# Four graph layers on one core: the source exponentials kept tile-innermost, their rows stored in one transfer and awaited head by head, with a new order table

## The chip, the cores and the metric

The kernel runs on one core of one Trainium2 chip, as one program. The time is the device time of that core in microseconds (us). An execution is timed as a whole; the profile comes from one profiled execution of the same program.

## What is computed

The input `x` is 16 graphs of 1024 nodes with 256 features, all float32, and one 1024 x 1024 adjacency matrix. Four layers follow each other, each as `x = x + layer(relu(layernorm(x)))`. Three of them (0, 1 and 3) are graph attention layers; layers 0 and 1 have one head of 256 features, layer 3 has four heads of 64. Layer 2 is a transformer block of eight heads of 32 features over the same mask, with two layer norms and a feed-forward part.

```
Wh = h @ W;  e_src = Wh @ a1;  e_dst = Wh @ a2
e   = leaky_relu(e_src[:, None] + e_dst[None, :], alpha)      # 1024 x 1024 per graph and head
att = softmax(where(adj > 0, e, -big), axis=-1)
out = elu(att @ Wh)                                            # layer 0: relu
```

The kernel never forms the exponential of a 1024 x 1024 matrix in these layers. Since the leaky relu is a maximum of two linear functions, `exp(e)` is, up to a factor that cancels in the softmax, `max(r[query], e2[key]) * e3[key]`, where `r`, `e2` and `e3` are exponentials of one number per node. `r` comes from the source part of the node ("source exponentials"), and the other two from its destination part.

## The kernel before

**Work units.** A "stage" is one layer of one graph, 64 in all. Nodes stand in `NT` = 8 tiles of 128 partitions. The stages are interleaved in a fixed list (`order`): in the middle of the run the cycle is layer 2 of graph b, layer 1 of graph b+1, layer 3 of graph b, layer 0 of graph b+2. While one stage does its main products on TensorE (PE), the next one is prepared.

**The way in.** For each tile: statistics of the norm (VectorE, DVE), the reciprocal root on GpSimd (POOL: `root`, L1051 and L1074), the normalised tile (ACT or DVE), then for every four tiles a PE transpose (`transpose_rows`, L1090) that ACT copies to `hT` (L1093). Products of `hT` with the weights follow on PE (`project`, L1097: `gat_values`, `two_values`, `queries_keys`).

**The source exponentials.** In an attention layer with H heads the product of a tile carries 3H extra columns; ACT turns them into exponentials in `e` (L1222, L1233), laid out as tile, then column: `e[p, t, c]`. `sources` then brings the rows `r` to all partitions: PE transposes `e` with its 8 x 3H columns (`tpr`, L1294), DVE copies the result to `rows_sb` (L1298), SyncE (SP) stores the H rows of `r` per tile to DRAM (`kept`; L1306 one transfer in one-head layers, L1309 eight transfers in layer 3), and SP loads them back, each row broadcast to 128 partitions (`r`; L1320 two halves of one row, L1325 four whole rows, two to a buffer). Only the first stage goes another way.

**The weights and the products.** DVE makes the weights `p = max(r, e2) * mask` (L1362, 512 queries for one-head layers; L1443, 1024 queries in layer 3, two heads to a pair), PE multiplies them with the values (L1379; in layer 3 `pair_item` with L1477 for values and L1501 for the sums). In layer 3 the weights of a pair of heads wait for one operation that loads both heads' rows. Layer 2 (`dot_item`) makes scores on PE (L1597), exponentials on ACT (L1611), the mask on DVE (L1619), values on PE (L1628), and adds two tiles of weights by a transfer of 1 MB that POOL issues (`gather`, L1645) before PE sums them (`totals`, L1658). POOL also issues the adding of constant rows in DRAM to `y` and `x` (`offset`, L1733); DVE's `finish` (L1797) waits for that of `y`.

**The order of the work.** The program records some 12,000 operations with their engine, an assumed cost, the operations they follow and the buffers they take and free. `play` then lays them out on five engines (and on a sixth line that stands for POOL's transfer queue) by a list scheduler: of the operations that could start soon, the one with the lowest key goes first. The key of each operation is read from `RANKS`, three characters to an operation, if its length is three times the number of operations; otherwise the program computes keys itself. What comes out is one fixed order of instructions for each engine, which the chip runs with semaphores between engines. So the assumed costs and `RANKS` decide only the order; they take no time on the chip.

**Shapes of products on PE.** Operations carry a `form`: 132 for the scores (32 rows of the array), 32 for products into 32-column parts (L1628, L1658, L1477, L1501), none for the rest. PE is slower by a fraction of a microsecond where two neighbours differ in form, and the scheduler's `SWITCH` stands for that.

Of the kernel before, what the change touches and what calls it, by code (L numbers as in the profile page):

```python
# [26 lines left out]
F32 = mybir.dt.float32  # L27
# [12 lines left out]
H2 = 8  # L40
# [7 lines left out]
    "#pO##/#29$4?#/<#._#28$Km#-d#9d#1K#/V#Yt#%>#$h$?-#+7#$u##6#(,#&-#$p#%O##O$As#;U#%U##.#$R#&L#,|$3z#':#-2#_.#'G#XJ"  # L48
    "$+<#'}#(o#)o#*I#)7#)<#*M#*e#$c$&3#$.#$P#UX#a@#$Q#qf$KH#$[#qV$,K##5#$6$?k##7#$>#*)#%=#$W#%Y#$T#$'#$w#'0#$@#%|#$n"
    "#$e$/]#$##$g$EX$A{#$i#qN#$L#${#ky#$($DA$H?#%/##:#&i$5&##J#%:#&P#%+#|w#%%#$l$#3#%@#`&#?m#i[##Y#$;#'&$4b#.n#lu#/m"  # L50
    "#Ns#Z1#)#$Mo#)x#N_#/g#,/#{(#'r#+/#(V#%{#$q#$Z##y##D#%$#$|#%N#&o#&y#-%#&O#$1#&H$9|##i#(1#Y:#-/#&F$+>#&w$:u#p1#(Y"
    "#%X#%W#%r$4R#'+#64#|-#'P#zk#&t#%M$Nz##}$NA$BA#)z#%o#'[#&X#XI#`a#*G$JF#(##+d#2Y#2C#d3#%a#%s#&D#&+#&G#&`#&Q#&7#%["
    "#%]#'g$7(#(K#*`$Ce#([#&f#']##m$NW#'>#*_$4<#'C#';#(J#%e#3}#&4#`8$@l#(Z#%w#&a#%.#1o#&]#.w#C[#/r#'Q#*z#(5#)C#-}#*F"
    "$=R#%V#'%$=^$.3#nf$K>#C0#%?#&J#z%#'W#)[#'X$EU$4[#'l#t)$4d#&=##;$2I#&?#)6$JX#Ag$4_#&##,5#&c$9.#(_#&:#$/#&k#(r#%5"
    "#[C#Z0#*H$>g#&g#rv$:-#&n#&|#-R#'($<P#6}#&;#)e#.t#%`#>o#%}#mY#&U##[#mt#'.$NG#&T#$*#%n$4J#&S$-($Ny#s6#IV#&s#*P#)]"
    "#m9$AU#(2##8#%0#$z#&3#&M#%T#$%$I##'8#/c#N$#*b#`J$Ds$L6#'/#v2#$m#4[#/Z#N'#<f#/B#'4#'v#'H#4<#Z>#)j$'9$J|##s#(&$L5"
    "#(S#Nz#+*$'8#'@#@o#)b#&h#(}#*4#*,#>w$+b#(s$M|#)k#,+#q+#%x#&6#'b#'m#Z?#(Q#(0#(T#)*#%K#o^#%J#*&$CO#+<#)$#)S$L=$&#"
    "#)P#*x$Di#H-$+^#l<#%##(t#&l#$}#<2#G`$.V$,.#$d#$]#&@#;_$C.##<#(^#(z#)/#E0#%6#$-#zs#$D#*6#,-#+K#,j#0n#:O#(U$@x#AU"
    "#yu#(/#)T#'J#'1#%)#(A#'M#&m#%*#kq$.6#qH$:m$5C#cs#9P$LP#m3#(.$5]$MO#UI#io$*]$8-#&(#(W#U|#/?#U:#'x$Cw$8*#)>#(G#]6"
    "#IN#UD$Ms#<9#,3#@R#{)#*E#Fq#)=$9C#)u#R2#EI#F-$7h$8t#q`$#^#GC#Gv#(v#)^#[x#$,##I$;V#SC#R=#)A#*}#$k#$&#]O$&H#T+$8i"  # L60
    "#Vy#)3##F$3c#@4#G;#0z#h$#(7#){#Jd#Fr#j=#K8$Eq#Fx#*B$-D#*3#+@#+e$G4#+E#gp#`[#.:#-$#)X#19#-x#0E#0F#)d#**#Y3#F?#F}"
    "#F3$EC#lb#*S#*@$@*#<<#Z=#mN#0K#<?#*##*$#*p#<=#Jc#Ft#0O#)p#)9#)}#W2#UG#y.#L[#1c#}h#*l#8O#.,##C#+L#*V#12#'t#^(#*="
    "#2d#hd#,A$IW#]h#ha#*^#*2#+x#V:#)8#)f#):$4I#(|#*n#`_#4M#,##51#0J#)|#+%#+9#)+#?C#`=#,x#UH#4+#*:#+:#&{#,h#&W#j%#*k"
    "#1D#+,$,d#.s$$[#,Q$Cr#Ol$3q#*U#Hg#)M$1?#+o#+i#+&#+>#c8#)W#lD#,W#+F#v%#,Z#*s#56#(L#/'$C>#+v#+w#*v#E|$EH#DE#,;#+H"
    "#e8#,m#+h#+0#E{#*A#<N#,`#,<$:W#d=#Y0#D`#+|$%,#13#-@#,9#Xb#d<#.N$+j#,k#,D#kK#D_#kJ#*K#,r$Ov#Im#Pm#-_#,K$)q#p@#ZP"
    "#0q#,s#,O$'*#0'$'x#p`#-P#qo#0]#-L#-,$)B#nX$)_#/+#-]#,w$)r#>0$,P#0i#-b$':#q8#+W#-O#b*#M8$+S#>/#+=#-N$(<$-w$'s#0w"
    "#,6#)h$1b#%p#+I#c^$)N#r$$-y#)V#+c$,1#1'#|v#'5#HJ#Th#qQ$2M#*Y$3@#,8#96#+s#(]#,d#+R#(a#.E#'7#-X#n##-5#q4#-f$H.#-B"
    "#%8#/S$>?#.h#&5#=/$I`#0V$-<#(<$4z#<S#ur#08#X]#'h#/k#^B$+&#$0#2%#XC$*i#9T#yy$(*#(;#0f#.O$Ba$B4#=y$5?#,^#bD$D.#*7"
    "#)I#5/#15#.u#9%#0e#/H#/=#{c$Bp#K>#0M#SK#vm$2U$0W#14#m_$0b#SN#}Y#Eu#2G#@W#2S#O]#,.#*C#?w#k|#1I#.T#-.$>V#jg#&r#8["
    "#em#pk#OQ#*O#-E#+N#iA#$4#>h#.*#.C$=M#'U#'B#hf#$?#&'#dq#.i#,>#_2#>R##4#'c#-V#$C$$x#'S$%?#)s#/:#8.#@w#0R#-8#,p#,o"  # L70
    "#,g#*{#0:#-^#_1#)l#^^#&x#/*#%g$32#e*#/x#*R#,e#-w#}m#./#.W#/E#`?#)Z#`>#-[#/(#&*$2N#0p#.5$B##'z#$9#.##.+#0d##P#-j"
    "$KI#-Y#0v#$V#mJ#1/#01#%l#-`#%R#.{#/{#0)#]q#:2#kX#:1#/X#(=$5;#1@#.-$>v#Lg#%q#:Y#0H#/w#$U#.z#0A#.y#1y$3f#92#Az#Oi"
    "#+t#RW#,7#(`#.A#06#,&#/F#0D#2+#.|#,u#0P##H#1?#u<#/,#4K#0r#.o#*w#2,#G4#=+#7>#u)#4:#]b#(B#uS#6V#@J#@+#7?#03#,Y#+6"
    "#-S#-s$Eu#4]#zH#=*#$j#.b#,2#9m#<o#}R#}c#+z#-m#Om#+k#&^#.V#'q$'&#0{#xk#+l#.r#1$$#'#CA#(E#+g$:l$3_#/##)i#/>#AA#3>"
    "#(@#.q#3#$/f#WR#2-#[{#W_#/^#BE#C|#6/$/w#)c$Cd#QZ#*]#,E#@;#*|#+u#?^#+1#+Z#;?#,:$Cv#,S#)Y#)n#-4#*r#lJ#3B#,q$)3#+C"
    "#(H$')$,@#qk#Pv#Id$Hj$&.#'e#+A$7m#.R#e0#0%#ta#->#,N#+G#,i$&{#&)#;Z$'+#)U$'(#-1#t:#+5$(n#&u#0G$(a$G6$%+#-o#Zg#7X"
    "#9F#9E#/O#-(#.7#/I#/2#0.#04#d%#YC#SR#1P#-y#??#@N#-k#HC$,3#Qc#00#=A##U$1;$-B$3)#7@#7U#4J#@Y#/A#/$#F##/Q$/F#7]#xs"
    "#=x#+b#'T#0|#*L#|B#.0#Wo#R%#uc#1F#1>$*D$MF$M6$6z#jr$?j#U<#/R$5[#/|#.U#-7#$E#0##B/#_G$2?#2]$/p#q3#W=$8?#W;##u#MK"
    "$FZ$/o#C>$;w$*?$*>$;j$/l$D$$,Q#d,#^h$)F$73#-M#.M#Jl#1G#cn#[5#QV#GQ$I]#/u$/u#0j$>w$C]$Nb#*i$M5$FE#D^#co#QK#1m#_|"
    "#6[#6L#^9#[##-G#^j#S6#MV#m*#/[#*d#-a#A,#7%#/z#/a#0x#-;#N{#6Z#-n#/Y#0S#.p#LF#3-#4c#4H#2<$DP#1%#1w#1Q#hg#5L#3F#1z"  # L80
    "#8C#0k#1A#0t#0>#44#4)#2F#3S#/G#1|#1u#02#1:#4=#0*#2E#1e#2e#5B#3q#1U#5D#3D$AE$3[#3I#4,#4##Bp#3E#C;$3o#Tz#L9#G<#ah"
    "$4|#Ge#,$#1V#4q#4S$%%#5C#3T#2'#2c#G##,y#4E$MY#'Y$:I#3<#1j#2W#1S#2D#F*#d[#2{#/h$#M#3j#E*#dd#Oo$:H#2v#3Z#3h#;f$A*"
    "#QW$/_#dO#i0$37#2h#Gs#18#Qo$Bm#2q#37#2r#r]#5c#O|#2H#4y#2u#O/#9.$G=$8@#Vq#lx$81#2w#R[#ux#LC$&h#to#1+#1Z#V|#*m$(:"
    "#mw$4v#?V$EW#3=#xi#h;#mn$8P#oH#$v##X#hh#dp#+M#n=#e|#Pe#8##$a#/%$8O#rR$4a#jV#$b##n#h6#rS$8L#n)#3k#P?$Ek#4Y##k#z'"
    "#oG$4$$0j#4w#3P#.=#jT#2I#jK#5@$3E#RS$BP#4$$LL#2s#u&#2n#49#$J#2b#2p#5-#2f#3G#1x#5*#PF#4s#Yk#5N#1R#6>#0b#5T#Tv#76"
    "#1&#6r#@}#U0$EE#*t#wT#:)$%*$#.#73#4_#Vn#&[#4m#2|#N&$-m#9##`E#/n#6X#Nq$J8#/0#/9#5Y$J:#22#;(#2}#?>#31#?=$'0#5;#Ac"
    "#[g#9Q#R>#'^#[$#9Z#5:#]5#^=#ny#Yq#EU#l;#Z8#6O#jL#5.#Z9#^m#@k##'$CS#k?#z&#>r#3$#4g#48#?[#23#N/#4;#PG$E2#4z##(#4-"
    "#;#$CK$N(#5'#4R#0[#LV#1[$(6#3_#Q&#s:#3s#3;#6H#KT$@7$'r#4?#0?$@;$Mi$5n#:@$G3#Pj$Ec#S,#3a$M/#')#17#u'#4/#4b#|r$Mh"
    "$@:#4d#Pc#0/#0g#7}#7;#3d$)##5z#cb#5^$FA#5U#Fv#4C#|z#6,$GB#XQ$Dp#[3#5s$3g#6-$2X#5Z#34#);#2k#69#f+#6?#$I#Z6$Au#5t"
    "#$N#79#6e#-##5)#6|#Rh#zx#6p#n2#7(#6a#$+#bQ#[e#5v#e{$#Y#3*#6o#5u#6Y#/3#eD#0+#7##6&#0<#XN$EJ#[6#9+#8w$7p#3&#wf#6`"  # L90
    "#-Z#6C#71$&D#9V#]Y#6s$(7#7k#5o#3/$L2#4|#Y^#4O#TZ#:b#]H#42#Yg#d(#c[#3x#vx#4A#7e#=B#6F#5J#68$*S#3]#4X#e3#:B#7L#7="
    "#&e#4o$In#4e#7c#8r#5O#6:#5##6j#fu#5+#|H#5X#8e#5d#5M$Io#0`#2R#5F#3g#8^#4T#7b#3{#tE#M^$A@$@X#:$#VP#4u#5f#J`$(3$Al"
# [527 lines left out]
def fast_path(tc, bad, x, adj, l0_w, l0_a, l1_w, l1_a, w_qkv, ln1_g, ln1_b, ln2_g, ln2_b, w1, b1, w2, b2, l3_w, l3_a, out):  # L620
# [13 lines left out]
    with ctx:  # L634
# [357 lines left out]
        class Stage:  # L992
# [38 lines left out]
            @property  # L1031
            def e(self):
                return self.eh.t

            @property
            def y(self):
                return self.yh.t
# [1006 lines left out]
```

## Time and profile before

| | |
|---|---|
| median of 3 runs | 4192.47 us (4190.18 to 4197.8) |
| profiled execution, as timed | 4190.34 us |
| its span, first to last instruction | 4188.6 us |
| mean granted TensorE clock | 0.995 |
| PE busy | 4085.4 us, 98% |
| DVE busy | 3174.7 us, 76% |
| ACT busy | 2319.6 us, 55% |
| POOL busy | 1207.9 us, 29% |
| transfers | 398.96 MB, 95 GB/s in the mean |

The span and the time as run differ by 1.7 us, and the profiled execution lies 2.1 us below the median. "Busy" counts an engine from the start to the end of each instruction; a PE that is busy may still be slowed by its clock, by a change of form or by a wait inside an instruction. In the profile a wait is put down to the engine that released it last.

### The profile page before, as it was taken

To read this page: it belongs to the slowest core of one execution; us is meant where nothing else is said; L and a number is where in the kernel's file an instruction comes from. 1 tells how busy PE (TensorE), PEld (TensorE's weight loads), DVE (VectorE), ACT (ScalarE), POOL (GpSimd) and SP (SyncE) were. 2 spreads that over 40 slices of the span, in tenths; PEclk is the share of its full clock that TensorE was granted. 3 is DMA by queue.
4 is the path that set the end of the run, shared out by engine and by line. 5 is a ranking of instruction groups with operands and counts; after the bars stand their busy time and mean duration, and the time that the engine had idled before them with its cause. 6 is when DMAs were issued, how large, how long until landed. Compare 5 with 4: busy or idle time off the path is not lost. (4 is left out here: it accounts for less than half of the span.)

```text
span 4188.6 us, 67542 instructions
## 1 busy us (share of the span) xinstructions
PE 4085.4 (98%) x25993; PEld 2158.0 (52%) x25993; DVE 3174.7 (76%) x5964; ACT 2319.6 (55%) x4235; POOL 1207.9 (29%) x2025
## 2 busy tenths in 40 slices
PE   8999999999999999999999999999999999999998
PEld 7735364553545535465454654536555365555433
DVE  7487867778676787777877778786787867768688
ACT  5564655646465464654647556474564645665452
POOL 2314231413314232141322313223142231423231
PEclk9999999999999999999999999999999999999999
DMA  3181914518154181641716327172361723554361
GB/s 125 31 167 31 186 36 106 106 46 171 36 126 97 37 170 41 132 95 46 156 37 149 79 63 144 31 166 62 78 130 51 162 46 90 114 113 98 85 122 47
DMA packets 106826, 398.96 MB, mean 95 GB/s; under 512 B 11528, under 2 KB 47744, under 8 KB 73728
## 3 DMA queue, kind: packets, MB, share of 16 engines
q0 software_dynamic: 46080, 302.01, 36.7%
q1 hardware_dynamic: 60000, 92.03, 6.7%
q8 instruction: 206, 3.38, 0.3%
q14 instruction: 124, 1.02, 0.1%
q10 hardware_dynamic: 416, 0.52, 0.0%
HBM read 107.87 MB, written 18.21 MB: 30 GB/s over the span
## 5 line engine op out<-in xcount | busy, mean ns | idle before, releaser
L1619 DVE TENSOR_TENSOR pe<-pe,mask 128x1024 f32<-128x1024 f32 x1024 | 1201.4, 1219 | 201.4 <-ACT pe L1611 196.8
L1611 ACT ACTIVATE pe<-sc 128x1024 f32<-128x1024 f32 x1024 | 996.4, 1023 | 322.2 <-PE sc L1597 241.0
L1379 PE MATMUL av<-v,p 128*128 128x257 f32 x4096 | 951.9, 382 | 10.2 <-ACT o L1402 6.0
L1379 PEld LDWEIGHTS av<-v,p 128*128 128x128 f32 x4096 | 761.6, 190 | 191.6 <-issue 48.7
L1443 DVE SCALAR_TENSOR_TENSOR p<-r,e,mask 128x1024 f32<-128x1024 f32 x512 | 623.1, 1274 | 121.7 <-DMA r<-kept 98.5
L1597 PE MATMUL sc<-qT,kT 32*128 32x512 f32 x4096 | 619.8, 640 | 5.1 <-ACT pm L1071 4.3
L1628 PE MATMUL acc<-pe,v 128*32 128x512 f32 x4096 | 539.9, 603 | 9.1 <-DVE pe L1619 6.1
L1074 POOL TENSOR_SCALAR rstd<-stats 128x1 f32<-128x1 f32 x512 | 166.6, 325 | 1157.9 <-ACT xn L1071 695.6
L1645 POOL DMA_DIRECT2D pe<-pe x256 | 224.9, 880 | 952.0 <-PE acc L1628 632.7
L1477 PE MATMUL acc<-p,v 128*32 128x512 f32 x4096 | 464.3, 595 | 0.0
L1597 PEld LDWEIGHTS sc<-qT,kT 32*128 32x128 f32 x4096 | 190.6, 183 | 379.7 <-issue 164.8
L1362 DVE SCALAR_TENSOR_TENSOR p<-r,e,mask 128x512 f32<-128x512 f32 x512 | 347.7, 742 | 30.5 <-DMA r<-kept 27.1
L1097 PE MATMUL pm<-l_wx,hT 128*128 128x259 f32 (+1 forms) x1536 | 366.6, 388 | 3.6 <-ACT hT L1093 3.0
L1075 POOL TENSOR_TENSOR rstd<-rstd,minus_half 128x1 f32<-128x1 f32 x512 | 331.9, 648 | 42.7
L1097 PEld LDWEIGHTS pm<-l_wx,hT 128*128 128x128 f32 x1536 | 286.2, 190 | 78.6 <-ACT hT L1093 13.3
L1658 PE MATMUL sums<-pe,pick 128*32 128x512 f32 x2048 | 268.5, 600 | 21.1 <-DMA pe<-pe 20.6
L1477 PEld LDWEIGHTS acc<-p,v 128*32 128x32 f32 x4096 | 129.8, 110 | 301.3 <-issue 288.8
L1628 PEld LDWEIGHTS acc<-pe,v 128*32 128x32 f32 x4096 | 96.6, 108 | 346.0 <-issue 200.8
L1051 POOL TENSOR_SCALAR rstd<-stats 128x1 f32<-128x1 f32 x256 | 138.5, 541 | 441.7 <-DVE stats L1048 438.7
L1501 PE MATMUL sums<-p,e 128*32 128x512 f32 x2048 | 242.3, 593 | 0.0
L1097 PE MATMUL pm<-hT,qkv_sb 128*128 128x512 f32 x512 | 228.0, 594 | 2.9 <-ACT hT L1093 2.8
L1052 POOL TENSOR_TENSOR rstd<-rstd,minus_half 128x1 f32<-128x1 f32 x256 | 221.8, 866 | 21.3
(122 smaller groups left out, 4147.9 us busy)
## 6 DMA issues: line engine op xcount, KB each, us to landing
pe<-pe POOLq DMA_DIRECT2D x256, 1024.0 KB, 8.8
r<-kept SPq DMA_DIRECT2D x64, 512.0 KB
x<-in_x_dram SPq DMA_DIRECT2D x32, 512.0 KB
x<-offsets POOLq DMA_DIRECT2D x32, 512.0 KB, 5.6
y<-offsets POOLq DMA_DIRECT2D x32, 512.0 KB, 6.9
out_dram<-x SPq DMA_DIRECT2D x64, 256.0 KB
r<-kept SPq DMA_DIRECT2D x62, 256.0 KB
edges<-in_adj_dram SPq DMA_DIRECT2D x8, 512.0 KB
```

Of the source, the lines that this page charges most:

```text
L1075: nc.gpsimd.tensor_tensor(rh.t, rh.t, minus_half, ALU.pow)
L1097: nc.tensor.matmul(dst, lhsT=lhsT[:, k, :], rhs=rhs[:, k, :], start=(k == 0), stop=(k == KC - 1))
L1362: nc.vector.scalar_tensor_tensor(ph.t[:, j % each, :], rh.t, s.e[:, j, H + h : H + h + 1], mask[:, j, cols], ALU.max, ALU.mult)
L1379: nc.tensor.matmul(avh.t[:, : s.hs + 1], lhsT=phs[part].t[:, j % each, i * P : (i + 1) * P], rhs=s.v[:, j, h, :], start=(j == 0), stop=(j ...
L1443: nc.vector.scalar_tensor_tensor(ph.t[:, hh, :], s.rh[hp].t[:, hh, :], s.e[:, j, col : col + 1], mask[:, j, :], ALU.max, ALU.mult)
L1477: nc.tensor.matmul(acc[n].t[(2 * hh + part) * W : (2 * hh + part + 1) * W, :], lhsT=s.v[:, jj, h, part * W : (part + 1) * W], rhs=p, start ...
L1501: both(lambda jj, n, hh, h, p: nc.tensor.matmul(sums.t[(2 * n + hh) * W : (2 * n + hh + 1) * W, 0, :], lhsT=s.e[:, jj, 2 * H + h : 2 * H + ...
L1597: nc.tensor.matmul(scs[pair].t[:, hh, :], lhsT=s.kh.t[r0 : r0 + D2, g, j * P : (j + 1) * P], rhs=s.qh.t[r0 : r0 + D2, g, cols], start=True ...
L1611: lambda pair=pair: nc.scalar.activation(part(pair), scs[pair].t, AF.Exp, scale=SCALE2),
L1619: lambda pair=pair: nc.vector.tensor_tensor(part(pair), part(pair), masks(), ALU.mult), [ex], tiles=True,
L1628: nc.tensor.matmul(head(acc, i), lhsT=s.v[:, j, g * QUAD + i, :D2], rhs=ph.t[:, i, :], start=(j == 0), stop=(j == NT - 1))
L1658: nc.tensor.matmul(head(sums, i), lhsT=pick[:, g, :], rhs=th.t[:, i, :], start=first, stop=last)
```

## The change

`e` is laid out column first: `e[p, c, t]`, so that the source columns of all tiles are the first 8H elements of each partition. `sources` transposes these 8H columns alone (8 instead of 24 columns with one head, 32 instead of 96 with four), copies that many rows and stores them in one transfer, from neighbouring partitions to neighbouring rows of `kept`. All readers of `e` go through a view with the old index order. The loads are recorded one by one: an operation without an instruction (`room`) takes the buffer, each row is a load of its own, and the weights of a head follow the load of that head. The number of operations grows from 12,154 to 12,280. Some assumed costs change (the root on POOL 1.4 to 1.55, the gather 5.2 to 5.6, the offsets 2.7 to 2.9, the delays of SP and of the transfer line), and `RANKS` is another table, of 36,840 characters.

```
 RANKS = (
...
-        DELAY = (0.2, 0.12, 0.14, 0.06, 2.0, 1.8)
+        DELAY = (0.2, 0.12, 0.14, 0.06, 1.8, 1.9)
...
-                    self.eh = buffer(small, "e", (P, NT, 3 * self.heads), "e")
+                    self.eh = buffer(small, "e", (P, 3 * self.heads, NT), "e")
...
             def e(self):
-                return self.eh.t
+                return self.eh.t.rearrange("p c t -> p t c")
...
-            r_op = op(POOL, 1.4, rank + 0.6, root, [m_op], ends=[mh])
+            r_op = op(POOL, 1.55, rank + 0.6, root, [m_op], ends=[mh])
...
-            turned = lambda: tph.t[: NT * 3 * H, 0, :P]
-            rows_h = buffer(small, "rows", (NT * 3 * H3, P), "rows_sb")
+            turned = lambda: tph.t[: H * NT, 0, :P]
+            rows_h = buffer(small, "rows", (H3 * NT, P), "rows_sb")
             a = op(
-                PE, 0.11, rank, lambda: nc.tensor.transpose(turned(), s.e.rearrange("p t c -> p (t c)"), ident), lead,
+                PE, 0.11, rank,
+                lambda: nc.tensor.transpose(turned(), s.eh.t[:, :H, :].rearrange("p h t -> p (h t)"), ident), lead,
                 takes=[tph], ends=[s.eh],
             )
             c = op(
-                DVE, 0.2, rank + 0.5, lambda: nc.vector.tensor_copy(rows_h.t[: NT * 3 * H, :], turned()), [a],
+                DVE, 0.2, rank + 0.5, lambda: nc.vector.tensor_copy(rows_h.t[: H * NT, :], turned()), [a],
                 takes=[rows_h], ends=[tph],
             )
...
-                kept.append(dram.tile([H3, NT, P], F32, tag="kept", name="kept"))
-                if H == 1:
-                    nc.sync.dma_start(out=kept[0][0], in_=rows_h.t[: 3 * NT : 3, :])
-                    return
-                for t in range(NT):
-                    nc.sync.dma_start(out=kept[0][:, t, :], in_=rows_h.t[3 * t * H : 3 * t * H + H, :])
+                kept.append(dram.tile([H3 * NT, P], F32, tag="kept", name="kept"))
+                nc.sync.dma_start(out=kept[0][: H * NT, :], in_=rows_h.t[: H * NT, :])
...
-            st = op(SP, 0.3 if H == 1 else 2.6, rank + 1.0, store, [c], ends=[rows_h])
+            st = op(SP, 0.3, rank + 1.0, store, [c], ends=[rows_h])
...
-                    for hh in range(2):
-                        nc.sync.dma_start(out=held.t[:, hh, :], in_=row(2 * part + hh).to_broadcast([P, N]))
+                    else:
+                        nc.sync.dma_start(out=held.t[:, hh, :], in_=row(2 * part + hh).to_broadcast([P, N]))
 
-                s.rops.append(op(
-                    SP, 0.4 if H == 1 else 0.9, rank + 4.0 + part, load, [st], takes=[held],
-                    delay=4.0 if H == 1 else 6.0,
-                ))
+                room = op(SP, 0.01, rank + 4.0 + part, lambda: None, [st], takes=[held], delay=0.0)
+                for hh in range(1 if H == 1 else 2):
+                    s.rops.append(op(
+                        SP, 0.4, rank + 4.0 + part, lambda hh=hh, load=load: load(hh), [room],
+                        delay=3.6 if H == 1 else 4.2,
+                    ))
...
-                    DVE, 1.195, first + 1.3 * hh, weights, [s.rops[hp], s.lead[j]] + ([s.pops[hp, j, 0]] if hh else []),
+                    DVE, 1.195, first + 1.3 * hh, weights, [s.rops[2 * hp + hh], s.lead[j]] + ([s.pops[hp, j, 0]] if hh else []),
...
-                    s.stores.append(op(SP, 0.8, rank_n + 6.0, store, [s.left[-1]]))
+                    s.stores.append(op(SP, 0.8, rank_n + 6.0, store, [s.left[-1]], delay=7.0))
...
-            gathered = op(QUEUE, 5.2, at[0] - 4.0, lambda: None, [issued], ends=[ph])
+            gathered = op(QUEUE, 5.6, at[0] - 4.0, lambda: None, [issued], ends=[ph])
...
-            return op(QUEUE, 2.7, rank, lambda: None, [issued])
+            return op(QUEUE, 2.9, rank, lambda: None, [issued])
```

## The prediction, made before the changed kernel ran

> **What bounds the kernel now.** I read the page's first part, then PE's own waits, then the overall list of waits, then a timeline of one place.
>
> ```profile
> span 4188.6 us, 67542 instructions
> ...
> PE 4085.4 (98%) x25993; PEld 2158.0 (52%) x25993; DVE 3174.7 (76%) x5964; ACT 2319.6 (55%) x4235; POOL 1207.9 (29%) x2025
> ...
> L1477 PE MATMUL acc<-p,v 128*32 128x512 f32 x4096 | 464.3, 595 | 0.0
> ...
> L1501 PE MATMUL sums<-p,e 128*32 128x512 f32 x2048 | 242.3, 593 | 0.0
> ```
>
> PE is the bound. It idles 103.2 us (4188.6 - 4085.4): 8.7 at the start, 16.1 after its last product but for a check (7.2 of it before that, 8.9 behind), so some 78 in the middle. No order can win more than that and what is lost inside busy time. The two layer 3 rows show 0.0 idle: PE never waits for the rows `r` there.
>
> ```profile
> PE sums L1658 <- DMA pe<-pe: 20.6, 29, 1.9
> PE pm L1097 <- ACT hT L1093: 14.2, 16, 1.4
> ...
> PE av L1379 <- ACT o L1402: 6.0, 9, 1.3
> PE tps L1677 <- ACT sums_sb L1668: 5.7, 5, 3.4
> ...
> DVE p L1443 <- DMA r<-kept: 98.5, 15, 11.0
> ```
>
> (total us, times, longest). PE's waits are small and many; the wait for `r` is DVE's. How it reaches PE is seen in one place, SP, DVE and PE around 2640:
>
> ```profile
> 2633.71 2.62 SPq L1309 DMA_DIRECT2D kept<-rows_sb  x8
> 2637.68 1.76 SPq L1325 DMA_DIRECT2D r<-kept  x4
> ...
> 2642.05 14.44 DVE L1443 SCALAR_TENSOR_TENSOR p<-r,e,mask 128x1024 f32<-128x1024 f32 x12 [6.72 <-DMA r<-kept]
> ...
> 2640.09 1.04 PE L1090 MATMUL tp<-ident,y 128*128 128x128 f32 x8
> 2642.28 3.72 PE L1097 MATMUL pm<-qkv_sb,hT 128*128 128x256 f32 x16 [1.16 <-ACT hT L1093]
> ...
> 2652.79 3.64 PE L1477 MATMUL acc<-p,v 128*32 128x512 f32 x32
> ```
>
> While the rows travel, PE is kept busy with products of the next layer 2 stage, and there a transpose is followed at once by the product that reads it: 1.16 us idle for the ACT copy between. The long trip is paid in such places.
>
> **Part 1: the row path.** In layer 3, from the copy's end (2633.69) to the first weight (2642.05): 8.36 us. Of it 2.62 are eight store issues, 1.35 the landing, 4.37 the loads. After: one store at 0.64 (what the one-head store L1306 takes to issue), 1.3 landing, and one head's 512 KB instead of two. A 256 KB load of a one-head stage that was waited for took 3.3 (issue 1152.14, weight 1155.48); I take 4.0, between. Sum 5.9, so 2.4 us earlier; in 15 waits 36 us of DVE idle. At PE this is worth nothing directly, since its rows above show 0.0 idle: products of other stages hide it. What it is worth through the order is in part 2. Only in the last stage, where DVE has no other stage's work, I give 1.0 of the 2.4.
>
> The transpose (0.27 us) and the copy (0.28) cost the same with 24 and 96 columns by their rows, so nothing is won there. SP issues 112 stores fewer and as many loads; it waits for 1277 us before L1306 alone, so no queue behind it is helped or hurt. `room` issues nothing, and holds SP where the load held it.
>
> Against the layout: [...] The trace has no such row; its nearest is ACT's L1222, 260 ns for 3 contiguous elements and 267 for 12: under 1 ns an element. By the rows the cost is 0; if each of 12 accesses cost as much again, 10 ns x 128 tiles, 1.3 us of an ACT that is busy 55%. [...] I take 0.
>
> **Part 2: the order.** It decides the result. I put the PE order of both programs side by side, as built. Counts are exact; prices come from the trace of before.
>
> (a) A product directly behind the transpose it reads: 10 places before, each idle 1.11 to 1.43 us; 5 after. -5 x 1.16 = -5.8. This is where the shorter trip goes: from `tpr` to layer 3's first product twelve stages in mid-run have 19 to 21 us of PE work before, 15.4 after, and none of these after has that pair.
>
> (b) Sums behind a gather (21.1 us of idle before all L1658 groups). PE work from the even tile's values to the sums, with the median duration of each operation: under 10.5 us in 74 of 256 cases before, 14 after. Mean idle by lead before: 0.18 us under 10.5, 0.085 to 11.5, 0.053 to 12.5, 0.037 to 15, 0.005 beyond. With the counts after (14, 53, 36, 82, 71): 12.4 us. -8.7.
>
> (c) A transpose of sums directly behind the sums it reads: 4 before, 1 after, 0.7 us each. -2.1.
>
> (d) Attention values that want a PSUM bank early (lead under 1.2 us): 16 before with 4.7 us idle, 17 after, two of them with no lead at all. +1.5.
>
> (e) Changes of form on PE: 1352 before, 1370 after. By start-to-start times without idle: into 32 +0.024, out of 32 +0.114, into none +0.105, out of none +0.091 us. By kind: none to 32 +13, 32 to none +7, 132 to none +9, none to 132 +3, 132 to 32 -10, 32 to 132 -4. Sum +3.5 us (the entries and exits of 132 are masked by waits; I put them at 0).
>
> (f) The start: the second transpose no longer stands behind three masks; DVE's `fill` work comes before the masks that wait 0.38 for their transfer. PE idles 2.5 us between 10 and 15 us now. -1.0, by estimate.
>
> (g) The few large stalls. Six stretches have a lowered clock:
>
> ```profile
> 1270.00:1280.00 10.00, 4.85 (x32) 2.07 (x32) 5.87 (x6) 4.67 (x6) 7.25 (x4) 0.83 0.46 93
> 2836.00:2846.00 10.00, 7.94 (x34) 4.89 (x35) 7.07 (x25) 7.37 (x22) 5.88 (x12) 0.83 0.42 87
> 3358.00:3368.00 10.00, 6.61 (x35) 5.29 (x28) 7.21 (x32) 6.96 (x22) 6.11 (x14) 0.83 0.00 1
> 3816.00:3827.00 11.00, 7.17 (x14) 2.51 (x13) 8.90 (x13) 0.58 (x1) 1.75 (x2) 0.69 0.72 140
> 4034.00:4045.00 11.00, 6.65 (x36) 1.82 (x32) 9.32 (x26) 6.93 (x15) 7.40 (x9) 0.69 0.41 83
> 4060.00:4070.00 10.00, 7.41 (x52) 1.78 (x44) 9.19 (x13) 0.58 (x1) 0.00 (x0) 0.83 0.01 2
> ```
>
> (the clock is third from the end.) The lost share, 4 x 1.7 + 2 x 3.4 = 13.6 us, comes on top of the idle time before. [...] the trace shows it also at 2837 (1.8 and 1.0 us idle close together) and 4060 (1.9 and 0.7). [...] In two of them (3358, 4034) DVE waited for an offset transfer issued 0.5 us behind a gather, with two gathers just before it in POOL's order: 9 of 32 such offsets before, 1 after. Their cost was 7.7 idle + 5.1 clock. But a new order makes stalls of its own that counts don't show. I take -2.5; bounds -13 (those two gone, none new) and +13.
>
> Sum: -1.0 -5.8 -8.7 -2.1 +1.5 +3.5 -1.0 -2.5 = -16.1 us. Against the profiled execution, 4190.3 - 16.1 = 4174.2; it lies 2.1 below the median of the runs, so I set the same difference against the median: 4192.5 - 16.1 = 4176.4.
>
> **Rivals.** *It comes out even (0.20).* The leads of (a) to (c) were bought with the 18 changes of form and with work pulled from elsewhere; ACT and DVE are queues too, and a product with enough lead by PE's work still waits if its copy stands behind a wait on ACT. For: ACT waited 38.2 us for `root` on POOL, up to 14.7 at once. Against: classes (a) to (d) hold some 40 of the 78 us in mid-run. If only half of (a) to (c) arrive (-8.3) and (e) stays, with (d), (f), the tail: -5.3, and new stalls of 5 us bring it to 4192.
>
> *Slower (0.08): the cover is too thin.* Twelve layer 3 stages go from 19.1 to 15.4 us of PE work while rows travel. Needed: 0.6 to the copy's end, the trip, 5.1 for the first four weights. At a trip of 5.9 that is 11.6. [...] one trip before, at 3806, took 11.5 us from copy to weight. From a trip of 9.7 on PE waits, 12 us per us beyond. To end 0.2% slower it would have to lose 24.5, a trip of 11.7 in every stage: 4201. Against: the layer 3 trips before, with eight stores and both heads' loads, took 8.4 to 11.0 us; less 2.4, that is 5.9 to 8.6.
>
> *More than forecast (0.06).* DVE has 36 us more; scores (L1597) take 54 us over their fastest pace in sum, through exponentials and masks that are late. A third of it: 4158.
>
> *The change does not do what it says.* The table would be ignored if its length were wrong. It is 36,840 = 3 x 12,280, and the built orders differ. No chance given.
>
> **Numbers.** The forecast (0.66) gives 4176.4. 0.2%, 8.4 us, is about what a measurement of this kernel can tell from no change: faster is below 4184. The forecast with (g) good or bad spans 4163 to 4190; its upper end, where it is within 0.2%, is counted with the even case. Faster 0.66 + 0.06 = 0.72, same 0.20, slower 0.08. The range takes in the even case and most of the larger gain: 4161 to 4194.
>
> **What would show it.** L1443 waiting for `r` some 60 us instead of 98.5, its gaps near 4.3 instead of 6.7; idle of L1658 near 12; L1097 behind `hT` near 8; PE busy within 5 us of 4085 and its idle time 15 to 20 less; fewer stretches under full clock. I am wrong if L1477 or L1501 show idle time (cover), if the idle time falls but busy time grows as much (form, clock), or if one or two stalls of over 4 us stand in new places.

## The result, and the profile after

The changed kernel takes 4163.47 us in the median of 4 runs (4160.7 to 4165.54), the kernel before 4195.14 beside it (4190.18 to 4197.81): 31.7 us less, ratio 0.9925 with a 95% interval of [0.9908, 0.9943]. The two profiled executions differ by 26.9 us of span, since that of before lies 4.8 under its median; what follows splits these 26.9.

The first part of the page, and PE's rows of layer 3 (busy us, mean ns | idle before):

```profile
span 4161.7 us, 67396 instructions
...
PE 4085.2 (98%) x25993; PEld 2155.8 (52%) x25993; DVE 3168.2 (76%) x5964; ACT 2321.0 (56%) x4235; POOL 1203.0 (29%) x2025
...
L1478 PE MATMUL acc<-p,v 128*32 128x512 f32 x4096 | 472.7, 593 | 1.9 <-ACT y L1493 1.3
...
L1502 PE MATMUL sums<-p,e 128*32 128x512 f32 x2048 | 253.0, 593 | 0.0
```

PE is busy as long as before (4085.4), so its idle time fell from 103.2 to 76.5. Equal busy time does not mean that nothing happened in it: stretches of lowered clock took 11.9 less (1.7 us against 13.6), changes of form some 3.6 more (an estimate from their count, at 0.02 to 0.11 us each by the trace of before), and the rest, some 8 us more, was not explained. The two rows of layer 3 are 8.4 and 10.7 us busier than before, but that is overlap with their neighbours: from start to start of the products, idle time left out, they take 1.5 less and 3.0 more. Of the 1.9 us of idle time before L1478, 0.6 are a wait for weights. PE's waits (total us, times, longest):

```profile
PE av L1380 <- ACT o L1403: 14.8, 15, 3.1
PE pm L1100 <- ACT hT L1096: 11.2, 10, 1.4
...
PE sums L1659 <- DMA pe<-pe: 5.0, 4, 1.8
...
PE tps L1678 <- ACT sums_sb L1669: 1.3, 4, 0.5
```

The sums behind a gather, the longest line before with 20.6, are down to 5.0; the attention values that wait for a bank (a piece of the memory that takes PE's results; ACT has to read it out first) have gone from 6.0 to 14.8 and now lead the list. The rows in the same place as the one shown of before, and DVE's wait for them in the list of all waits:

```profile
2624.73 0.91 POOL L1734 DMA_DIRECT2D x<-offsets  x1 [0.93 <-ACT y L1138]
...
2627.16 0.32 SPq L1309 DMA_DIRECT2D kept<-rows_sb  x1
...
2630.20 1.74 SPq L1324 DMA_DIRECT2D r<-kept  x4
2634.14 2.48 DVE L1444 SCALAR_TENSOR_TENSOR p<-r,e,mask 128x1024 f32<-128x1024 f32 x2 [7.00 <-DMA r<-kept]
...
2641.38 3.64 PE L1478 MATMUL acc<-p,v 128*32 128x512 f32 x32
```

```profile
DVE p L1444 <- DMA r<-kept: 104.9, 17, 8.1
```

The eight issues (2.62 us) became one of 0.32, and yet DVE waits no less (98.5 before). The store's landing grew: from its end at 2627.48 to the first load 2.72 us pass, against 1.35 before. An offset transfer of 512 KB had been issued 2.4 us ahead. PE's first product of the stage now starts 14.8 us behind `tpr` (2626.55); in the mid-run stages of before it started 18.3 to 21.4 us behind it.

In mid-run there is one stretch with a lowered clock, 0.50 for 3.41 us from 351.21, where before had six. It lies in the first of these windows; the second, at about the place where before had one at 3358, has the full clock (columns: window, length, busy time and count by engine, clock third from the end):

```profile
348.00:358.00 10.00, 8.47 (x32) 6.52 (x32) 3.71 (x16) 4.89 (x13) 4.41 (x11) 0.83 0.01 2
...
3350.00:3360.00 10.00, 9.19 (x54) 6.37 (x53) 7.05 (x30) 8.76 (x27) 7.62 (x17) 1.00 0.01 2
```

### The profile page after: what moved, and what is told of

Its sections match the earlier page's. It is cut to its first block, busy times and chain, and to the rows that moved or that the text cites. A ratio compares the mean times of both kernels' runs of the same rounds, so it can differ in the third digit from the quotient of the medians.

```text
span 4161.7 us, 67396 instructions
## 1 busy us (share of the span) xinstructions
PE 4085.2 (98%) x25993; PEld 2155.8 (52%) x25993; DVE 3168.2 (76%) x5964; ACT 2321.0 (56%) x4235; POOL 1203.0 (29%) x2025
## 4 chain that ended last, share of the span: by engine, by line
PE 83%; DVE 7%; DMA 3%; ACT 3%; issue 2%; POOL 1%; SPq 0%; ACTq 0%; POOLq 0%; DVEq 0%
PE av L1380 20%; PE pm L1100 20%; PE sc L1598 11%; PE acc L1478 10%; PE acc L1629 9%; PE sums L1502 5%; PE sums L1659 4%; DVE pe L1620 3%; PE tp L1093 3%; DMA pe<-pe 2%; DVE p L1444 1%; ACT pm L1074 1%; ACT pe L1612 1%; PE tpo L1678 1%; PE tpv L1541 1%
## 5 line engine op out<-in xcount | busy, mean ns | idle before, releaser
L1380 PE MATMUL av<-v,p 128*128 128x257 f32 x4096 | 953.1, 383 | 17.1 <-ACT o L1403 14.8
L1444 DVE SCALAR_TENSOR_TENSOR p<-r,e,mask 128x1024 f32<-128x1024 f32 x512 | 622.5, 1274 | 113.6 <-DMA r<-kept 104.9
L1478 PE MATMUL acc<-p,v 128*32 128x512 f32 x4096 | 472.7, 593 | 1.9 <-ACT y L1493 1.3
L1078 POOL TENSOR_TENSOR rstd<-rstd,minus_half 128x1 f32<-128x1 f32 x512 | 337.0, 658 | 42.6
L1478 PEld LDWEIGHTS acc<-p,v 128*32 128x32 f32 x4096 | 132.9, 110 | 298.6 <-issue 274.6
L1502 PE MATMUL sums<-p,e 128*32 128x512 f32 x2048 | 253.0, 593 | 0.0
L1154 ACT ACTIVATE xn<-x,stats 128x256 f32<-128x256 f32 x256 | 123.4, 504 | 227.4 <-DVE stats L1051 223.3
L1055 POOL TENSOR_TENSOR rstd<-rstd,minus_half 128x1 f32<-128x1 f32 x256 | 225.6, 881 | 21.3
```

The costliest lines, as they stand in the source:

```text
L1078: nc.gpsimd.tensor_tensor(rh.t, rh.t, minus_half, ALU.pow)
L1380: nc.tensor.matmul(avh.t[:, : s.hs + 1], lhsT=phs[part].t[:, j % each, i * P : (i + 1) * P], rhs=s.v[:, j, h, :], start=(j == 0), stop=(j ...
L1444: nc.vector.scalar_tensor_tensor(ph.t[:, hh, :], s.rh[hp].t[:, hh, :], s.e[:, j, col : col + 1], mask[:, j, :], ALU.max, ALU.mult)
L1478: nc.tensor.matmul(acc[n].t[(2 * hh + part) * W : (2 * hh + part + 1) * W, :], lhsT=s.v[:, jj, h, part * W : (part + 1) * W], rhs=p, start ...
L1502: both(lambda jj, n, hh, h, p: nc.tensor.matmul(sums.t[(2 * n + hh) * W : (2 * n + hh + 1) * W, 0, :], lhsT=s.e[:, jj, 2 * H + h : 2 * H + ...
```

## The experiments

The kernel before ran beside each group of runs, and ratios are against it, with 95% intervals in brackets. "Trip" is the median time from the end of the copy to `rows_sb` to the first weight of a layer 3 stage, over the 13 or 14 stages where DVE waited for the rows. Line numbers shift by a few between kernels.

### Which part carries the gain: order, path, or both

The new order with the old layout, transpose and eight stores (against the changed kernel):

```diff
-                    self.eh = buffer(small, "e", (P, 3 * self.heads, NT), "e")
+                    self.eh = buffer(small, "e", (P, NT, 3 * self.heads), "e")
...
-                nc.sync.dma_start(out=kept[0][: H * NT, :], in_=rows_h.t[: H * NT, :])
...
+                for t in range(NT):
+                    nc.sync.dma_start(out=kept[0][:, t, :], in_=rows_h.t[3 * t * H : 3 * t * H + H, :])
```

> The changed kernel with the row path of before: e laid out tile first, all 3H columns transposed, eight strided stores in layer 3. Every engine's order of instructions is that of the changed kernel, but for SP's extra stores. Theory 'order': the gain lies in the order of instructions and not in the row path; the time stays within 5 us of the changed kernel's, 4160 to 4169 us. In layer 3 the trip from the copy to the first weight grows from 7.7 to between 8.4 and 9.7 us; PE needs 0.6 + trip + 5.1 us of cover and has 15.4, so at most a few tenths of a us per stage show. Rival 'path': the shorter trip itself earns a part; then this kernel loses 10 us or more of the 32.

Measured: 4190.03 us (4185.62 to 4192.94), ratio 0.9985 [0.9977, 0.9992]. The order alone brings 6 of 32 us, so the theory that the order does it all fell. The trip is 9.35 us. First the page's row of the layer 3 products, then PE's wait:

```profile
L1482 PE MATMUL acc<-p,v 128*32 128x512 f32 x4096 | 488.5, 594 | 6.7 <-DVE p L1448 5.1
```

```profile
PE acc L1482 <- DVE p L1448: 5.1, 8, 1.1
```

Only 5.1 us show as a wait; 15.8 more are inside busy time (472.7 after). Matched operation by operation, PE's times from the start of one product to the start of the next are 29.2 us longer than in the changed kernel: mainly 11.3 at `acc`, 7.8 at the sums of layer 3 and 4.8 at transposes. By stage, 21.9 us lie in thirteen layer 3 stages, 0.5 to 3.2 in each, and 4.1 in the last.

The other half, the new layout, transpose and one store in the kernel before with its own order:

```diff
-                    self.eh = buffer(small, "e", (P, NT, 3 * self.heads), "e")
+                    self.eh = buffer(small, "e", (P, 3 * self.heads, NT), "e")
...
+                nc.sync.dma_start(out=kept[0][: H * NT, :], in_=rows_h.t[: H * NT, :])
```

> The kernel before with the new row path alone: tile-innermost layout, H x 8 columns transposed, one store; its own order on every engine. Theory 'order': within 4 us of before, 4191 to 4199 us, since PE has 19 us of products in front of it whatever the trip takes; DVE's wait for r in layer 3 falls from 98.5 us by 1 to 2.4 us per stage. Rival 'path': 10 us or more faster than before.

Measured: 4195.36 us, ratio 0.9999 [0.9991, 1.0008]. The trip fell to 6.22 us and PE took nothing of it: from first weight to first product went from 10.8 to 13.3 us. So the path is worth 0 in the old order, the order 6 with the old path, both together 32. One makes the other usable. (The loads stay paired in this run; what awaiting them head by head is worth is measured below.)

### What in the path the new order needs

Three kernels change the path of the changed kernel alone. Store cut into eight by rows:

```diff
-                nc.sync.dma_start(out=kept[0][: H * NT, :], in_=rows_h.t[: H * NT, :])
+                n = 8 if H > 1 else 1
+                for i in range(n):
+                    nc.sync.dma_start(
+                        out=kept[0][i * H : i * H + H * NT // n, :], in_=rows_h.t[i * H : i * H + H * NT // n, :]
+                    )
```

> The changed kernel with its layout, its order and its loads head by head, but in layer 3 the store of the 32 rows is cut into eight transfers of four rows. It splits the loss of 26.6 us that the old path made in the new order. Theory A (issue time on SP): eight issues take 2.6 us instead of 0.3, the landing behind them 2.2 instead of 3.0, so the trip goes from 7.7 to about 9.3 us, the weights end about 4 to 5 us before PE's first product where 5.1 is needed, and nearly all of the loss comes back: 4180 to 4192 us. Theory B (waiting for both heads' rows at once, or the 96-column transpose and its copy, made the loss): 4163 to 4170 us.

Measured: 4174.95 us (4173.72 to 4179.93), ratio 0.9958 [0.9945, 0.9972], between the two theories. The trip is 7.62, as after: each head's load needs only two of the eight transfers, and their landing lay beside the other issues. The thirteen stages lost 3.7 us together, and the two of them in which the trip grew most (5.9 to 7.8 us at 368, 7.1 to 9.2 at 1615) lost 4.0. The last stage, where no offset transfer delays the store, lost 4.0 as well: trip 6.8 instead of 5.5. So here too the loss stands where the rows came later.

Both heads' rows in one load:

```diff
-                        nc.sync.dma_start(out=held.t[:, hh, :], in_=row(2 * part + hh).to_broadcast([P, N]))
+                        if hh == 0:
+                            both = kept[0][2 * part * NT : 2 * (part + 1) * NT, :].rearrange("t q -> (t q)").rearrange("(o f) -> o f", o=1)
+                            nc.sync.dma_start(out=held.t.rearrange("p h q -> p (h q)"), in_=both.to_broadcast([P, 2 * N]))
```

> The changed kernel with one store, its order unchanged, but in layer 3 both heads' rows of a pair come in one transfer of 1 MB, so that the weights of the first head wait for both. Theory A (the store's issues carry the gain): from load to weight 4.0 to 4.5 us, at most 0.5 us more trip where 1.4 us of room is left: 4163 to 4169 us. Theory B (awaiting head by head carries it): the loss of the old path comes back in good part, 4178 us or more, with load to weight over 5 us.

Measured: 4162.25 us (4161.29 to 4165.0), ratio 0.9926 [0.9912, 0.9939]: nothing lost. Load to weight took 4.61 instead of 4.03, the trip 8.2. Awaiting the rows head by head is worth nothing measurable.

Eight stores cut by tiles, so that every load needs all eight:

```diff
-                nc.sync.dma_start(out=kept[0][: H * NT, :], in_=rows_h.t[: H * NT, :])
...
+                for t in range(NT):
+                    nc.sync.dma_start(
+                        out=kept[0].rearrange("(h t) q -> h t q", t=NT)[:, t, :], in_=rows_h.t[t : H * NT : NT, :]
+                    )
```

> The changed kernel with its layout and its short transpose, but the 32 rows of layer 3 stored by eight transfers of the other cut: each carries one tile of all four heads, to rows eight apart. In the cut by rows (4175.0 us) a head's load needed only two of the eight transfers, so their landing lay beside the other issues and the median trip stayed at 7.6 us; here, as in the old path, every load needs all eight. Theory A (eight issues and then the landing of the last make the loss of the old path): landing near 2.2 us behind the last issue, trip 9.0 to 9.5, 1 to 3 us lost in each layer 3 stage: 4183 to 4192 us. Theory B (the rest of the old path's loss comes from the layout and the transpose with 24 or 96 columns): as with the cut by rows, 4172 to 4178 us.

Measured: 4207.78 us (4202.85 to 4212.6), ratio 1.0039 [1.0026, 1.0053]: slower than before, beyond theory A. In its timeline, beside the page's row of the products:

```profile
2653.62 4.80 SPq L1313 DMA_DIRECT2D kept<-rows_sb  x8
...
2659.95 1.74 SPq L1330 DMA_DIRECT2D r<-kept  x4
...
2664.03 2.48 DVE L1450 SCALAR_TENSOR_TENSOR p<-r,e,mask 128x1024 f32<-128x1024 f32 x2 [10.43 <-DMA r<-kept]
...
2667.84 4.33 PE L1484 MATMUL acc<-p,v 128*32 128x512 f32 x30
...
2674.95 3.20 PE L1484 MATMUL acc<-p,v 128*32 128x512 f32 x26 [0.62 <-DVE p L1450]
```

```profile
L1484 PE MATMUL acc<-p,v 128*32 128x512 f32 x4096 | 504.6, 594 | 12.3 <-DVE p L1450 10.6
```

Each issue takes 0.60 us here instead of 0.35. The old path stored to the same rows, eight apart, from neighbouring partitions, at 0.35; what differs at 0.60 is the source's partitions, eight apart here. The trip is 10.55. Layout and short transpose are those of the changed kernel, so they do not carry the gain by themselves. What the loss follows is the time at which the rows arrive. The timeline also shows where the loss falls. Against the changed kernel this stage loses next to nothing at its first product, 0.7 us within the first few microseconds, 1.5 within 12 and 3.3 within 40: DVE, which started late with its weights of 1.24 us each and waits 1.12 once more for rows, no longer keeps ahead, and PE waits in the middle of its products.

The kernels in one table (medians in us; "lost" is PE's start-to-start time over the changed kernel, thirteen stages + last stage; span is that of the profiled execution):

| path, in the new order | issue | store end to load | load to weight | trip | first weight to PE | lost | span |
|---|---|---|---|---|---|---|---|
| changed kernel | 0.32 | 2.98 | 4.03 | 7.7 | 6.9 | | 4161.7 |
| one load per pair | 0.32 | 3.26 | 4.61 | 8.2 | 6.2 | 1.0 - 0.5 | 4163.1 |
| eight stores by rows | 2.84 | 0.65 | 4.13 | 7.6 | 6.8 | 3.7 + 4.0 | 4171.9 |
| old path | 2.84 | 2.21 | 4.21 | 9.4 | 5.0 | 21.9 + 4.1 | 4190.9 |
| eight stores by tiles | 4.81 | 1.45 | 4.25 | 10.6 | 3.8 | 35.8 + 6.0 | 4204.7 |

The time that SP spends on issuing is not the cause by itself: cut by rows it is that of the old path, 2.84 us, and 7.7 us are lost instead of 26.

### Where the gain lies: the gathers

The gather adds only two of its four heads, in the order before and in the new one; the sums of the other heads then leave the odd tiles out.

```diff
-                    out=th.t.rearrange("p i q -> p (i q)"), in_=ph.t.rearrange("p i q -> p (i q)"), accum_op=ALU.add
+                    out=th.t[:, : QUAD // 2].rearrange("p i q -> p (i q)"), in_=ph.t[:, : QUAD // 2].rearrange("p i q -> p (i q)"), accum_op=ALU.add
```

> The kernel before with gathers of half the bytes: only the first two of four heads of a quad are added, so half the sums leave out the odd tiles. Order unchanged. Theory 'gather': the sums' wait for the gather (20.6 us of PE idle) is a true cost of the old order; nearly all of it goes, with the offset transfers queued behind gathers landing earlier too: 18 to 30 us faster than before, 4165 to 4177 us. Rival 'other waits take its place': less than 8 us faster.

> The same halving of the gathers in the changed kernel, in its order. Theory 'gather': its order already gives the gathers time (5.0 us of idle left), so 4 to 8 us faster than the changed kernel, 4155 to 4160 us; the distance between the two orders shrinks from 32 to about 15 us with gathers halved in both. Rival: both kernels move by the same amount, and the gathers are not where the orders differ.

Measured: 4148.39 us in the old order, ratio 0.9888 [0.9871, 0.9904], and 4144.35 in the new, 0.9877 [0.986, 0.9893]. Half the gather (4.6 us to land instead of 8.8) is worth 48 us before and 19 after, more than the 18 to 30 and 4 to 8 that were expected. With it the two programs differ by 4 us instead of 32. So some 28 of the 32 us depend on the length of the gathers, which the new order covers better. These runs do not split that into waits and clock: with the old order and half the gathers the lowered stretches in mid-run fall from six to two as well.

The new order with the old path and halved gathers:

> The new order with the old row path, and the gather adding only the first two of the four heads of its two tiles (the sums of the other two leave the odd tiles out). With halved gathers the changed kernel took 4144.4 and the kernel before 4148.4 us. Cover theory: the old path's issues still make its trip over 9 us in the new order, so about as much is lost as with full gathers (26.6 us): 4165 to 4172 us. Rival (the loss needs the full gathers, whose transfers delay the rows or meet the late weights): 4146 to 4155 us.

Measured: 4165.8 us (4164.78 to 4168.26), ratio 0.9934 [0.992, 0.9947], 21 us over the changed kernel with halved gathers (24 by the ratios, each taken beside its own runs of the kernel before). So late rows cost about as much with short gathers as with long ones (26.6): the cover theory holds, its rival falls.

### The offset transfers

They are left out in both programs, so the constant rows are not added.

```diff
-                nc.gpsimd.dma_start(out=(s.y, xs[s.b])[which][:, ts, :], in_=offsets[which], accum_op=ALU.add)
+                return
```

> The kernel before without the 64 transfers that add constant rows to y and x (the adding of those rows is left out; order unchanged otherwise). Theory 'offsets behind gathers': the two stalls at 3358 and 4034, 7.7 us of idle and 5.1 us of lowered clock, go, and the sums behind gathers land a little earlier: 12 to 20 us faster than before, 4176 to 4184 us. Rival 'the stalls have another cause': the clock still drops there and the gain is under 6 us.

> The changed kernel without those 64 transfers. In its layer 3 stages the store of the rows lands 3.0 us after its issue where an offset transfer was issued 2 us earlier, and 1.2 us where none was; without them the trip from copy to first weight should fall from 7.7 to about 6 us. Theory 'cover': 15.4 us of PE work covers a trip of up to 9.7, so the shorter trip is worth nothing: 2 to 6 us faster than the changed kernel, 4158 to 4162 us. Rival 'no cover left': the old row path in this order cost 27 us for 1.7 us more trip, so 1.7 us less earns some 15 to 20 us: 4143 to 4148 us.

Measured: 4171.38 us in the old order (ratio 0.9951 [0.9934, 0.9967], 22.6 less), 4148.46 in the new (0.9895 [0.9878, 0.9911], 15.0 less than the changed kernel). The old order gains more than its range of 12 to 20. The two stalls that the theory named, at 3358 and 4034, are gone, and the time lost to the lowered clock fell from 13.6 to 8.5 us. In PE's waits of the old order without offsets the sums still wait:

```profile
PE sums L1658 <- DMA pe<-pe: 16.5, 25, 2.4
```

(20.6 before.) Of the six lowered stretches those at 1276 and 4065 remain, and a new one stands at 3588. In the new order the trip falls from 7.7 to 5.76, the store lands in 1.15:

```profile
2622.81 0.32 SPq L1309 DMA_DIRECT2D kept<-rows_sb  x1
2624.26 1.74 SPq L1324 DMA_DIRECT2D r<-kept  x4
...
2628.54 2.48 DVE L1444 SCALAR_TENSOR_TENSOR p<-r,e,mask 128x1024 f32<-128x1024 f32 x2 [5.76 <-DMA r<-kept]
```

Yet the thirteen stages gain 6.6 us of the 15, and 5.2 of that in two places where the kernel with one load per pair also stood better. Most of the rest is idle time in front of the attention values that follow sums of layer 2 and wait for a bank (17.1 to 12.7), and 3.2 us behind PE's last product; the sums' own wait for gathers does not fall (5.0 to 6.2). So neither number that I gave for the new order (2 to 6, or 15 to 20 through the cover) describes it: the total is near that of the second, the place is not. At 7.7 us the trip is short enough: 1.9 us less of it won 1.4 us in the other eleven stages together.

Adding the rows on POOL from SBUF instead, which leaves nothing out, as a possible better version:

```diff
...
-                nc.gpsimd.dma_start(out=(s.y, xs[s.b])[which][:, ts, :], in_=offsets[which], accum_op=ALU.add)
+                to = (s.y, xs[s.b])[which][:, ts, :]
+                nc.gpsimd.tensor_tensor(to, to, offset_sb[:, which, :].unsqueeze(1).to_broadcast([P, TH, C]), ALU.add)
...
```

> The changed kernel with the constant rows held in SBUF and added by an instruction on POOL (128 x 1024) instead of a transfer that POOL issues; all else and the order unchanged, the result complete. Theory: POOL is busy 29%, so if the add takes under 3 us it lands earlier than the transfer's 5.3 to 5.5 us and leaves the transfer engines to the gathers: near the kernel without offsets, 2 to 6 us faster than the changed kernel. Rival: the add is slow [...], and the roots and gathers behind it on POOL come late: 5 us or more slower than the changed kernel.

Measured: 4200.15 us (4196.04 to 4206.25), ratio 1.0017 [1.001, 1.0025]: 37 us worse than the changed kernel. The group of the additions, and PE's wait behind it:

```profile
L1735 POOL TENSOR_TENSOR y<-y,offset_sb 128x1024 f32<-128x1024 f32 x32 | 91.6, 2863 | 42.8 <-PE tp L1093 35.4 <-ACT pe L1612 7.3
...
L1735 POOL TENSOR_TENSOR x<-x,offset_sb 128x1024 f32<-128x1024 f32 x32 | 75.4, 2357 | 26.7 <-ACT y L1138 26.7
```

```profile
PE av L1380 <- ACT o L1403: 27.4, 15, 3.4
```

An addition holds POOL 2.4 to 2.9 us, where the issue of the transfer held it 0.9; DVE's busy time grows by 68.5 us. The trip is short here (5.7 us), so the rows are not the reason. About half of the loss stands in the clock: ten lowered stretches in mid-run cost 22.2 us, where the changed kernel has one of 1.7. Six of the ten stand at a wait of these attention values of 2.6 to 3.4 us. No version that beats the changed kernel and leaves nothing out was found.

### The costs and the table

The changed kernel with the assumed costs of before for the root, the gather, the offsets, the stores of the output and the delays, which gives another built order from the same table:

```diff
-        DELAY = (0.2, 0.12, 0.14, 0.06, 1.8, 1.9)
+        DELAY = (0.2, 0.12, 0.14, 0.06, 2.0, 1.8)
...
-            gathered = op(QUEUE, 5.6, at[0] - 4.0, lambda: None, [issued], ends=[ph])
+            gathered = op(QUEUE, 5.2, at[0] - 4.0, lambda: None, [issued], ends=[ph])
```

> The changed kernel and its table of keys, but with the assumed costs of before (root 1.4, gather 5.2, offsets 2.7, delays 2.0 and 1.8, no delay of the output stores). The same keys then give another order. By the same count of PE work between producer and consumer, the shortfalls sum to 409 us in it, against 121 before and 96 after. Theory 'leads in the order set the time': far slower than both, 4300 us or more. Rival 'the keys carry the order, the costs matter little': within 20 us of the changed kernel.

Measured: 4414.24 us (4411.01 to 4417.47), ratio 1.053 [1.0509, 1.0551]. Among PE's waits:

```profile
PE sums L1659 <- DMA pe<-pe: 40.3, 32, 2.8
PE acc L1478 <- DVE p L1444: 30.8, 12, 8.8
```

Table and costs belong together. In the counts of the built orders the direction holds too: summed over PE's operations, the lead that is short of what their inputs take is 409 us here, against 121 before and 96 after.

## Why the prediction was right, and where its sum was off

The direction held, and the place in part: nothing comes from the shorter transfer by itself, but the order alone brings 6 of the 32 us, and the rest needs the shorter path under it. The result lies 2.5 us inside the lower end of the range, so it owes that to the range's width. The sum was half of the result: -16.1 forecast, -31.7 by medians, -26.9 by the two profiles. By its own terms, as the profiles show them:

| term | forecast | measured |
|---|---|---|
| (a) products behind their transpose | -5.8 | -2.7 (14.9 to 12.2 idle, all of these products) |
| (b) sums behind a gather | -8.7 | -16.0 (21.1 to 5.1 idle) |
| (c) transposes of sums | -2.1 | -4.4 (6.4 to 2.0) |
| (d) attention values, bank | +1.5 | +6.9 (10.2 to 17.1) |
| (e) changes of form | +3.5 | +3.6, not measured: the counts at the forecast's prices |
| (f) start | -1.0 | -1.0 |
| (g) large stalls and clock | -2.5 | -11.9 by the clock |

The right column adds up to -25.5, but that it comes so near the 26.9 is luck. Idle time fell by another 9.4 us that stand in no row, mainly at values, transposes and scores of layer 2, where three of the four wide stalls of before stood. The fourth, 3.4 us at 3362, is most of what (c) lost. Against that, busy time hardly changed, though (e) and (g) together take 8.3 us from it; so some 8.1 us of busy time came in by ways that no row has.

**The row path (part 1).** "At PE this is worth nothing directly" held exactly in the old order. The size failed at one step: one store at 0.64 and a landing of 1.3. The store takes 0.32 to issue, but lands in 2.98 us in the median, since an offset transfer runs ahead of it in most stages (1.15 without offsets); 7.7 us came out instead of 5.9, and DVE's wait stayed at 104.9 instead of 60. The 1.0 us for the last stage was 0 in the old order (PE's times there differ by 0.06), while in the new one 1.3 us of trip costs 4.0.

**The thin cover.** The rival's mechanism is real, and it is the one that the experiments show: 0.5 us lost at a trip of 8.2, 26 at 9.4 and 42 at 10.6. My threshold (9.7) was too late and its price (12 us per us) too low: between the last two it is (41.8 - 26.0) / 1.2 = 13, between the first two (26.0 - 0.5) / 1.2 = 21. I had asked when the *first* product waits; what waits is the products 6 to 40 us later. I gave it 0.08 since the trip was to be 5.9 to 8.6. It came out inside that, at 7.7, though by a shorter issue and a longer landing than I took.

**The gathers (b).** The mis-sized step is "mean idle by lead before" used as a price after. It is no property of the lead alone: 14 sums with under 10.5 us of lead cost 0.10 each after, where 0.18 was taken, and the 82 from 12.5 to 15 us cost 0.37 together where 3.0 was taken. A gather issued within 5 us behind an offset transfer does land later (11.9 us in the median before, against 8.7 elsewhere), but such places are as many after (9) as before (10). Taking all offsets away in the old order brings this wait only from 20.6 to 16.5. So the offsets explain at most some 4 of the 7.3 us that the term had too few, and the rest is open. The offsets of `y` that stand close behind two gathers, 9 of 32 before, were to be 1; in the trace of after, 5 of them start within 1 us of a gather. They still land sooner, in 5.5 us instead of 6.9.

**The stalls (g).** I took a fifth of a stake of 13.6 us because "a new order makes stalls of its own". It made few: over 3 us in mid-run there is one where there were four, and one lowered stretch instead of six. The four runs in the new order with other paths had two each ahead of the last stage (1.7 us lost per stretch of 3.41 at a clock of 0.50). Nor is it the chance of one execution: the granted clock was 0.993 to 0.996 in every execution of the kernel before and 0.998 in all four of the changed kernel. Few gathers late, few wide stalls, little clock lost: (b) and (g) move together, and were counted as if apart. Halving the gathers in the old order, which took the stretches from six to two, shows the same tie.

**The others.** (a) and (d) were wrong by 3 and 5 us the other way: their counts had PE's work in front of a product, but not what stands before the awaited copy on ACT. That this is the reason was not tested. "More than forecast" gave 4158, near the result, but by DVE's free time, which did not come; the excess of the scores did fall, from 54.3 to 42.6 us, with idle time and clock in it that other rows have too. The layout, which I put at 0, has a price on ACT; the rows of before and after:

```profile
L1222 ACT ACTIVATE e<-pm,rstd 128x12 f32<-128x12 f32 x128 | 29.3, 267 | 43.3 <-PE pm L1097 36.9 <-POOL rstd L1075 2.5 <-DVE v L1246 2.2
```

```profile
L1225 ACT ACTIVATE e<-pm,rstd 128x12 f32<-128x12 f32 x128 | 31.2, 279 | 57.9 <-PE pm L1100 47.6 <-DVE v L1249 4.3 <-POOL rstd L1078 3.5
```

The new layout alone, in the old order, has 279 ns as well, and the old layout in the new order 267. So 12 ns x 128 = 1.5 us of ACT go to it, about the 1.3 that I had as its upper bound, an estimate of mine from the 267 ns for 12 elements; at 4195.36 us against 4196.39, the kernel with that path in the old order shows none of it.

## What to carry to other kernels

A shorter transfer that is hidden is worth nothing until the order is drawn tighter around it; here it was then worth 26 of 32 us. Test a path and an order together and each alone, or the interaction (0, 6, 32 us) stays unseen. A mean wait taken from the old order was not the price in the new one, even at the same lead (0.18 against 0.10 us), and the clock is to be counted with the stalls that it falls behind (13.6 us before, 1.7 after). Whether a cover is too thin is not seen at the first product alone: here it was lost later, where the engine that feeds the products had lost its lead.

## What the runs showed of the hardware

**A small store beside a large transfer.** A 16 KB store lands in 1.15 us in the median of the changed kernel without offset transfers, and in 2.98 in the changed kernel, where one runs ahead of it in most stages. In the timeline of the changed kernel, in a stage without such a neighbour:

```profile
3695.73 0.32 SPq L1309 DMA_DIRECT2D kept<-rows_sb  x1
3697.24 1.75 SPq L1324 DMA_DIRECT2D r<-kept  x4
```

1.19 us lie between, against 2.72 at 2627. What delays the store was not separated here.

**A stall and the clock.** The attention values at the same place of the order wait for a bank in the changed kernel and in three of its variants. The changed kernel, then the one with one load per pair, each with its window:

```profile
1291.22 2.01 PE L1380 MATMUL av<-v,p 128*128 128x257 f32 x8 [3.11 <-ACT o L1403]
```

```profile
1290.00:1300.00 10.00, 8.78 (x53) 6.89 (x54) 7.91 (x30) 8.05 (x25) 7.94 (x18) 1.00 0.01 2
```

```profile
1294.32 3.44 PE L1382 MATMUL av<-v,p 128*128 128x257 f32 x8 [3.44 <-ACT o L1405]
```

```profile
1290.00:1300.00 10.00, 6.56 (x33) 3.81 (x23) 7.53 (x34) 5.98 (x19) 6.00 (x12) 0.83 0.00 1
```

After 3.11 us of idle the clock stays whole; after 3.44, 3.50 (old path) and 3.86 (eight stores by rows) it falls (0.83 in the mean of the 10 us that hold the 3.44), and each such stretch costs 1.7 us more. It is not the length of the stall alone that decides, though. In the kernel with the additions on POOL the same attention values wait 3.12 us, and the clock falls:

```profile
2345.30 3.65 PE L1380 MATMUL av<-v,p 128*128 128x257 f32 x8 [3.12 <-ACT o L1403]
```

```profile
2340.00:2350.00 10.00, 6.88 (x31) 3.51 (x30) 7.59 (x32) 4.94 (x15) 6.07 (x12) 0.83 0.00 0
```

The eight products behind it take 3.65 us, against 2.01 behind the 3.11. In the trace of before the lowered stretches of mid-run start at 1275.98, 2839.28, 3361.52, 3818.91, 4037.36 and 4064.67, the five behind the first 458, 611, 745, 809 and 817 times 3.4133 us later, and show a clock of 0.50 for one or two such lengths. Counted in intervals of this length from a lowered start of the same trace, the 3.11 us of the changed kernel fall into two, 1.76 and 1.35; the 3.12 us, with all eight products behind them slowed, into one. With PE's idle time counted by interval, from 20 us to PE's last product, all six intervals of before at full clock with over 1.9 us of idle (2.04 to 3.41) were followed by a lowered one, and none of the 15 with 1.15 to 1.82; in the changed kernel one of 18 with 1.11 to 1.80 was, with 1.53. Why that one and not the others was not shown. Four of the six stretches of before followed a wait of 3.4 to 4.6 us; the two that followed shorter pauses close together, at 2837 and 4060, have 2.04 and 2.05 us of idle in one interval.

**POOL as an adder.** 2.4 to 2.9 us for 1024 elements per partition, against 1.22 us for a DVE multiplication of that size. DVE's busy time grew by 2% beside it; why was not separated.
